# A selective scan that takes two channel tiles per step instead of one

## The chip, the cores and the metric

The kernel runs on one core of a Trainium2 chip. Its metric is device time in microseconds: three runs of the kernel before took 5609.75, 5609.93 and 5616.93 us (median 5609.93). One further execution was recorded by the hardware profiler; its trace is what the tables below are read from.

The core's engines work side by side, each on its own list of instructions, in that list's order: PE multiplies matrices into PSUM, DVE works element by element, ACT does functions of one input (exponentials, copies), POOL issues the scattered transfers, SP issues nearly all others. They wait for each other by semaphores.

## The reference

One decoder block over x of 8 sequences of 512 tokens of width 512, all in float32, with a layernorm after each of three parts: a state-space layer, cross attention (16 heads of 32, keys and values from a context), and a mixture of 32 experts (4 per token, 640 places each) with a shared expert. The change is in the state-space layer. Per channel d of 1024 and state n of 16:

```python
dt = softplus(dt @ dt_proj_w + dt_proj_b)
dA = exp(A * dt)                      # decay, per channel, state and token
dBx = dt * B * x_main                 # what a token adds
h = dA_t * h + dBx_t                  # the recurrence over the tokens
y_t = sum over n of h * C_t
out = res_scale * ((y + x_main * D) * silu(z)) @ out_proj_w + x
```

A = -exp(A_log); B and C come from a product of x_main with x_proj_w, and x_main is a causal convolution of four taps followed by silu.

## The kernel before, in words

`layers` works in 16 chunks: 8 sequences of two chunks of T = 256 tokens. A chunk has 1024 channels in 8 tiles c of 128, taken as four pairs q (tiles 2q and 2q+1); the 16 states are in four groups g of NG = 4. A step is one (q, g, i), i being the tile of the pair, so a chunk has 32 steps k and the program 512. A tile of a step is laid out so that each partition holds two channels j by two states m; `dt` and `dt*x` are copied into that form by the DMAs of `prepare` (the tiles `both`).

One step does this, in program order:

- `bcast` (L374), in the first step of a pair: four transfers that fetch the next group's B and C rows to all partitions (tiles `bc`, four buffers).
- `carry` (L439): takes an h buffer, 4 rows of 257, from a pool of four, and ACT copies the last state (or zeros, `nothing`) into column 0.
- `decays` (L433) for the *next* step: four exponentials of 256 columns on ACT into one of two `das` tiles.
- `scan` (L446): on DVE the product of `dt*x` with B over 1024 columns (L449), then one `tensor_tensor_scan` through all 4 x 257 columns (L453; column 0 of each decay row is 0, so each row starts from its carried state), and, in the first chunk of a sequence, a copy of the last column to `state` (L455).
- work of other parts (below).
- `collect` (L457): DVE multiplies h by C in place (L470), and PE sums over states with four products with the matrix `twice` into `py` (L474).

The other work is hung on step numbers: `back` (the output projection of the chunk before) at k = 1 and 2, `gate_x` at 3 to 6, `prepare` of the next pair at k % 8 == 3 (PE product, seven ACT operations, four DVE operations, two more on ACT, eight transfers `both<-dt` and `both<-dtx`), `convolve` at 12, 15, 18 and 21, `x_proj` of the next chunk at 24. Beside these runs a list `side`: the attention and routing of the sequence before (`units`), with weights in time that spread it evenly over 64 steps. Each piece has up to three parts (PE, then ACT or DVE, then more), and a part is emitted when the next piece has been (`do`, `settle`).

So the program order is written by hand, with weights. The compiler's list scheduler then reorders each engine's list within the dependencies, so products of a later step may come before other work. At run time each engine keeps its list's order. A pool's buffer is handed out again when its last reader has finished; for h that is PE's L474.

After `layers` come `experts` and a last layernorm (`finish`), which the change does not touch.

Of the kernel before, what the change touches and what calls it, by code (L numbers as in the profile page):

```python
# [7 lines left out]
F32 = mybir.dt.float32  # L8
I32 = mybir.dt.int32
U8 = mybir.dt.uint8  # L10
AF = mybir.ActivationFunctionType
# [5 lines left out]
P = 128  # L17
# [9 lines left out]
T = 256  # L27
# [54 lines left out]
def layers(ctx, tc, a, x1d, filld, based, xbuf):  # L82
# [73 lines left out]

    conv_tail = cp.tile([P, CC, 3], F32, name="l_conv_tail")
    state = cp.tile([P, CC, NST // NG, NG], F32, name="l_state")
    nothing = cp.tile([P, NG, 1], F32, name="l_nothing")
    nc.gpsimd.memset(nothing, 0.0)  # L160
    das = [cp.tile([P, NG, T + 1], F32, name=f"l_da{i}") for i in range(2)]
    for da in das:
        nc.gpsimd.memset(da[:, :, 0:1], 0.0)

# [23 lines left out]
        channel_multiplier=0,  # L188
    )

    early = cp.tile([P, SC, E], F32, name="l_early")
    nc.gpsimd.iota(
        early, pattern=[[0, SC], [-1, E]], base=E, channel_multiplier=0, allow_small_or_imprecise_dtypes=True
    )
    first = cp.tile([P, SC, E], F32, name="l_first")
    nc.gpsimd.iota(
        first, pattern=[[0, SC], [CAP, E]], base=-SLOTS, channel_multiplier=0, allow_small_or_imprecise_dtypes=True
    )

    taken = cp.tile([P, SC + 1, E], F32, name="l_taken")  # L200
    nc.gpsimd.memset(taken, 0.0)
# [172 lines left out]
    def bcast(f, g):  # L374

        got = []
        for r0 in (g * NG, NST + g * NG):
            t = bcp.tile([P, NG // 2, T], F32, tag="bc", name="bc")
            for r in range(2):
                n0 = r0 + r * NG // 2  # L380
                nc.sync.dma_start(
                    t[r * HP : (r + 1) * HP], f["scr"][n0 : n0 + NG // 2, :].partition_broadcast(HP)
                )
            got.append(t.unsqueeze(1).to_broadcast([P, 2, NG // 2, T]))
        return got

    def prepare(q, f):
# [42 lines left out]

        return exponentials

    def decays(c, g, dt, da):  # L433

        for n in range(NG):
            j, m = n // 2, n % 2
            nc.scalar.activation(da[:, n, 1:], dt[:, c % 2, j, :], AF.Exp, scale=aneg[:, c, j, g, m : m + 1])  # L437

    def carry(t, c, g):  # L439

        last = state[:, c, g].unsqueeze(2)
        h = p3.tile([P, NG, T + 1], F32, tag="h", name="h", bufs=4)
        nc.scalar.copy(h[:, :, 0:1], last if t else nothing)  # L443
        return h

    def scan(t, c, g, dtx, bc, da, h):  # L446

        steps = h.rearrange("p (j m) t -> p j m t", j=2)[:, :, :, 1:]
        nc.vector.tensor_tensor(  # L449
            steps, dtx[:, c % 2].unsqueeze(2).to_broadcast([P, 2, NG // 2, T]), bc[0], ALU.mult  # L450
        )
        flat = h.rearrange("p n t -> p (n t)")
        nc.vector.tensor_tensor_scan(flat, da.rearrange("p n t -> p (n t)"), flat, 0.0, ALU.mult, ALU.add)  # L453
        if t < S // T - 1:
            nc.vector.tensor_copy(state[:, c, g].unsqueeze(2), h[:, :, T : T + 1])  # L455

    def collect(c, g, h, bc, py, f):  # L457


        if g == 0:  # L460
            for j in range(2):
                nc.tensor.matmul(
                    py[j * HP : (j + 1) * HP, c % 2, :],
                    ident[:, j * HP : (j + 1) * HP],
                    f["xs"][c // 2][:, c % 2, :],
                    start=(c % 2 == 0),
                    stop=False,
                )
        steps = h.rearrange("p (j m) t -> p j m t", j=2)[:, :, :, 1:]
        nc.vector.tensor_tensor(steps, steps, bc[1], ALU.mult)  # L470
        for m in range(NG // 2):
            for j in range(2):
                s = (g, m, c % 2)
                nc.tensor.matmul(  # L474
                    py[j * HP : (j + 1) * HP, c % 2, :],
                    twice,
                    h[:, j * 2 + m, 1:],
                    start=False,
                    stop=(s == (NST // NG - 1, NG // 2 - 1, 1)),
                )  # L480
# [63 lines left out]
    def choose(b, x2t, pl, st):  # L544
# [13 lines left out]
        square = [P, SC, G, G]  # L558
        other = gs.unsqueeze(2).to_broadcast(square)
        own = gs.unsqueeze(3).to_broadcast(square)  # L560
        eq = gm.tile(square, F32, tag="g_eq", name="g_eq")
        nc.vector.tensor_tensor(eq, other, own, ALU.is_equal)
        nc.vector.tensor_tensor(eq, eq, lower.unsqueeze(1).to_broadcast(square), ALU.mult)
        gt = gm.tile(square, F32, tag="g_gt", name="g_gt")
        nc.vector.tensor_tensor(gt, other, own, ALU.is_gt)
        nc.vector.tensor_tensor(gt, gt, eq, ALU.add)
        nc.vector.tensor_reduce(rank.unsqueeze(3), gt, AX.X, ALU.add)
# [455 lines left out]
    for i, (b, t) in enumerate(chunks):  # L1023
# [8 lines left out]
        for k, (q, g, ci) in enumerate(steps):  # L1032
            if ci == 0:
                if (q, g) != (CC // 2 - 1, NST // NG - 1):
                    bcn = bcast(f, (g + 1) % (NST // NG))
                else:
                    bcn = bcast(nf, 0) if after else None
            h = carry(t, 2 * q + ci, g)

            if k + 1 < len(steps) or after:  # L1040
                nq, ng, ni = steps[(k + 1) % len(steps)]
                decays(2 * nq + ni, ng, (f if k + 1 < len(steps) else nf)["ready", nq][0], das[(n + 1) % 2])
            scan(t, 2 * q + ci, g, f["ready", q][1], bc, das[n % 2], h)
            n += 1
            if k % 8 == 0:
                if k:
                    gated(q - 1, f, py)
# [9 lines left out]
            if k == 7:  # L1057
                dry()
                silu(f["zs"])
            if k % 8 == 3:  # L1060
                if q + 1 < CC // 2:
                    do(prepare, q + 1, f)
                elif after:
                    do(prepare, 0, nf)
# [354 lines left out]
```

## Time and profile before

| what | us |
|---|---|
| median of three runs | 5609.93 |
| profiled execution, time | 5620.06 |
| profiled execution, span of the core | 5617.3 |
| mean granted TensorE clock | 0.934 of full |

Busy time of each engine by stage (us):

| window | PE | DVE | ACT | POOL | granted clock |
|---|---|---|---|---|---|
| 0 to 280 (constants, first chunk) | 166.79 | 215.60 | 135.35 | 21.44 | 0.83 |
| 280 to 3640 (scan with the side work) | 2899.31 | 3029.36 | 1901.24 | 242.17 | 0.93 |
| 3640 to 5617 (last attention, experts) | 1822.51 | 1106.57 | 555.57 | 282.46 | 0.96 |

How to read what follows: DVE is VectorE, ACT ScalarE, POOL GpSimd, SP the queue that issues transfers; PE's weight loads stand apart as PEld. A group's line names line, engine, operation, output and inputs by the program's tile names, shapes, and how often; behind it busy us, the mean ns of one, the engine's idle us just before them, and what ended most of it. A line of waits gives who waited for whom, the total us, how often, the longest. Matmuls are recorded twice each (two passes). A busy engine is not always at its best rate, and the idle time of an engine that is not the bottleneck costs nothing.

### The profile page before, as it was taken

The numbers are of one execution on the slowest core, as the hardware profiler recorded it, in microseconds if no ns is written. First come the engines' busy times: TensorE is split into PE (matmuls) and PEld (weight loads), VectorE is DVE, ScalarE is ACT, GpSimd is POOL, SyncE is SP. The second block draws the span as 40 slices with busy tenths as digits, with TensorE's granted clock in tenths as the row PEclk, the third lists the DMA queues.
The fourth block names the chain that finished last, engine by engine and source line by source line (L and its number), as shares of the span: only waits on it lengthen the run. The fifth ranks groups of instructions, "written<-read, shape, count | busy, mean of one in ns | idle before, by whom it ended". The sixth has DMA issues, their size and how long they took to land. (4 is left out here: it accounts for less than half of the span.)

```text
span 5617.3 us, 60406 instructions
## 1 busy us (share of the span) xinstructions
PE 4888.6 (87%) x19752; PEld 2725.6 (49%) x19752; DVE 4351.5 (77%) x5738; ACT 2592.2 (46%) x5480; POOL 546.1 (10%) x424
## 2 busy tenths in 40 slices
PE   5667888888888988888888898879899999999994
PEld 3333344434433434443443443333577777777773
DVE  5988888989889998898989899854555655555554
ACT  4454555655556555565545656523122222222223
POOL 0000002001100200200010020010111111111111
PEclk8778999999999999999999999989899999999997
DMA  6777345434534534543463453431444444444444
GB/s 207 215 219 201 99 129 177 128 112 130 189 107 113 190 107 122 177 132 106 124 204 94 125 183 110 115 118 45 137 124 126 124 124 119 125 126 124 120 117 138
DMA packets 560426, 769.83 MB, mean 137 GB/s; under 512 B 135754, under 2 KB 268394, under 8 KB 560112
## 3 DMA queue, kind: packets, MB, share of 16 engines
q1 hardware_dynamic: 522608, 680.70, 40.2%
q0 software_dynamic: 33280, 76.90, 7.0%
q10 hardware_dynamic: 4224, 8.39, 0.4%
q8 instruction: 156, 2.56, 0.2%
q14 instruction: 158, 1.29, 0.1%
HBM read 508.68 MB, written 165.05 MB: 120 GB/s over the span
## 5 line engine op out<-in xcount | busy, mean ns | idle before, releaser
L437 ACT ACTIVATE l_da<-both,l_aneg 128x256 f32<-128x256 f32 x2048 | 888.4, 499 | 801.8 <-DVE h L453 759.7
L453 DVE TENSOR_TENSOR_SCAN h<-l_da,h 128x1028 f32<-128x1028 f32 x512 | 1171.2, 2295 | 48.5 <-ACT h L443 26.4
L474 PE MATMUL py<-h,l_twice 128*64 128x256 f32 x4096 | 628.1, 420 | 217.4 <-DVE h L470 217.3
L449 DVE TENSOR_TENSOR h<-both,bc 128x1024 f32<-128x1024 f32 x512 | 619.2, 1216 | 97.2 <-PE py L474 45.4
L470 DVE TENSOR_TENSOR h<-h,bc 128x1024 f32<-128x1024 f32 x512 | 623.5, 1220 | 6.0
L474 PEld LDWEIGHTS py<-h,l_twice 128*64 128x64 f32 x4096 | 295.3, 147 | 587.6 <-DVE h L470 260.7
L766 PE MATMUL ps_s<-l_ka,l_qa 64*128 64x512 f32 x1024 | 317.1, 699 | 142.9 <-DVE mx L768 142.7
L1199 PE MATMUL ps_h<-xT,w 128*128 128x320 f32 x1536 | 435.6, 433 | 0.0
L1279 POOL DMA_INDIRECT based<-y,xe x160 | 250.5, 1565 | 1317.2 <-ACT y L1302 579.9
L768 DVE TENSOR_REDUCE mx<-ps_s 128x2 f32<-128x1024 f32 x256 | 310.8, 1217 | 83.7 <-PE ps_s L766 82.9
L1220 DVE TENSOR_TENSOR hT<-ps_h,p 128x320 f32<-128x320 f32 x128 | 62.9, 492 | 374.7 <-PE ps_h L1199 374.6
L1199 PEld LDWEIGHTS ps_h<-xT,w 128*128 128x128 f32 x1536 | 292.4, 191 | 118.4 <-issue 0.8
L792 PE MATMUL ps_t<-l_qa,l_ka 64*128 64x512 f32 x1024 | 302.0, 654 | 15.8 <-ACT eT L796 11.9
L796 ACT ACTIVATE eT<-ps_t 128x1024 f32<-128x1024 f32 x256 | 259.1, 1013 | 111.9 <-PE ps_t L792 111.5
L808 PE MATMUL po<-eT,l_va 128*64 128x512 f32 x1024 | 279.2, 623 | 23.0 <-ACT raw L820 19.0
L1199 PE MATMUL ps_h<-t,s 128*128 128x320 f32 x1024 | 286.1, 432 | 0.0
L641 POOL DMA_INDIRECT xbuf<-x2t,dest x128 | 216.7, 1693 | 622.1 <-DVE dest L635 583.7
L305 PE MATMUL ps_z<-xnT,wm 128*128 128x256 f32 x1024 | 246.3, 395 | 31.2 <-DMA wm<-in_in_proj_w 28.4
L503 PE MATMUL po<-wm,zs 128*128 128x512 f32 x512 | 246.7, 634 | 13.0 <-DMA wm<-in_out_proj_w 8.5
L703 PE MATMUL ps_p<-x2T,wa 128*128 128x512 f32 x512 | 244.7, 627 | 11.1 <-DVE hT L883 9.1
L305 PE MATMUL ps_x<-xnT,wm 128*128 128x256 f32 x1024 | 245.3, 393 | 1.4 <-ACT xnT L294 1.1
L305 PEld LDWEIGHTS ps_z<-xnT,wm 128*128 128x128 f32 x1024 | 196.2, 196 | 83.7 <-ACT l_da L437 27.1
(225 smaller groups left out, 7397.0 us busy)
## 6 DMA issues: line engine op xcount, KB each, us to landing
bc<-scr SPq DMA_DIRECT2D x1024, 128.0 KB
w<-in_w SPq DMA_DIRECT2D x96, 1024.0 KB
wm<-in_in_proj_w SPq DMA_DIRECT2D x128, 512.0 KB
xbuf<-zero SPq DMA_DIRECT2D x32, 1362.5 KB
xe<-xbuf SPq DMA_DIRECT2D x32, 1362.5 KB
both<-dt SPq DMA_DIRECT2D x256, 128.0 KB
both<-dtx SPq DMA_DIRECT2D x256, 128.0 KB
wm<-in_out_proj_w SPq DMA_DIRECT2D x64, 512.0 KB
```

The source lines that it names most:

```text
L305: nc.tensor.matmul(ps[:, i, :], w[:, dc, i * P : (i + 1) * P], f["xnT"][:, dc, :], start=(dc == 0), stop=(dc == DC - 1),)
L437: nc.scalar.activation(da[:, n, 1:], dt[:, c % 2, j, :], AF.Exp, scale=aneg[:, c, j, g, m : m + 1])
L449: nc.vector.tensor_tensor(steps, dtx[:, c % 2].unsqueeze(2).to_broadcast([P, 2, NG // 2, T]), bc[0], ALU.mult)
L453: nc.vector.tensor_tensor_scan(flat, da.rearrange("p n t -> p (n t)"), flat, 0.0, ALU.mult, ALU.add)
L470: nc.vector.tensor_tensor(steps, steps, bc[1], ALU.mult)
L474: nc.tensor.matmul(py[j * HP : (j + 1) * HP, c % 2, :], twice, h[:, j * 2 + m, 1:], start=False, stop=(s == (NST // NG - 1, NG // 2 - 1, 1)),)
L766: nc.tensor.matmul(ps[:, j, :], qa[r, lt * P : (lt + 1) * P], ka[r, :], start=True, stop=True)
L768: return lambda: nc.vector.tensor_reduce(mx[:, lt, :].unsqueeze(2), ps, AX.X, ALU.max) and None
L792: nc.tensor.matmul(ps[:, j, :], ka[r, kc * P : (kc + 1) * P], qa[r, :], start=True, stop=True)
L796: nc.scalar.activation(eT, ps, AF.Exp)
L808: nc.tensor.matmul(po[j * 2 * HD : (j + 1) * 2 * HD, :], va[:, kc, i, j * HD : (j + 2) * HD], eT[:, j, :], start=(kc == 0), stop=(kc == SC ...
L1199: nc.tensor.matmul(ps, w[:, n, r * P : (r + 1) * P], x[:, n, :], start=not more and n == 0, stop=n == 1, skip_group_check=more,)
```

## The change

A step's scan work is done once for both tiles of a pair. The h tile and the two decay tiles hold 8 rows of 257 instead of 4; h has two buffers instead of four. In the first of a pair's two steps `carry` copies 8 columns, `decays` writes the eight decays of the *next pair's* step, and `scan` does one product with B over 2048 columns, one scan through 2056 and one copy of 8 states. The second step has none of these. `collect` stays as it was, once for each tile, on its half of h, after that step's other work. `prepare` moves from k % 8 == 3 to k % 8 == 2. To make room, the constants `early` and `first` are held once and read as broadcasts over the four row tiles, and `g_eq` and `g_gt` of the routing take one buffer of the pool "row" in place of two of their own.

```diff
-    das = [cp.tile([P, NG, T + 1], F32, name=f"l_da{i}") for i in range(2)]
+    das = [cp.tile([P, 2 * NG, T + 1], F32, name=f"l_da{i}") for i in range(2)]
...
-    early = cp.tile([P, SC, E], F32, name="l_early")
+    early = cp.tile([P, E], F32, name="l_early")
...
+    early = early.unsqueeze(1).to_broadcast([P, SC, E])
...
-    def decays(c, g, dt, da):
-
-        for n in range(NG):
-            j, m = n // 2, n % 2
-            nc.scalar.activation(da[:, n, 1:], dt[:, c % 2, j, :], AF.Exp, scale=aneg[:, c, j, g, m : m + 1])
-
-    def carry(t, c, g):
-
-        last = state[:, c, g].unsqueeze(2)
-        h = p3.tile([P, NG, T + 1], F32, tag="h", name="h", bufs=4)
-        nc.scalar.copy(h[:, :, 0:1], last if t else nothing)
+    def decays(q, g, dt, da):
+
+        for i in range(2):
+            for n in range(NG):
+                j, m = n // 2, n % 2
+                nc.scalar.activation(
+                    da[:, i * NG + n, 1:], dt[:, i, j, :], AF.Exp, scale=aneg[:, 2 * q + i, j, g, m : m + 1]
+                )
+
+    def carry(t, q, g):
+
+        h = p3.tile([P, 2 * NG, T + 1], F32, tag="h", name="h", bufs=2)
+        nc.scalar.copy(h.rearrange("p (i n) t -> p i n t", i=2)[:, :, :, 0], last(q, g) if t else none)
         return h
 
-    def scan(t, c, g, dtx, bc, da, h):
-
-        steps = h.rearrange("p (j m) t -> p j m t", j=2)[:, :, :, 1:]
+    def last(q, g):
+        return state[:, 2 * q : 2 * q + 2, g]
+
+    def scan(t, q, g, dtx, bc, da, h):
+
+        steps = h.rearrange("p (j m) t -> p j m t", m=NG // 2)[:, :, :, 1:]
+        both = [P, 4, NG // 2, T]
         nc.vector.tensor_tensor(
-            steps, dtx[:, c % 2].unsqueeze(2).to_broadcast([P, 2, NG // 2, T]), bc[0], ALU.mult
+            steps,
+            dtx.rearrange("p i j t -> p (i j) t").unsqueeze(2).to_broadcast(both),
+            bc[0].to_broadcast(both),
+            ALU.mult,
         )
         flat = h.rearrange("p n t -> p (n t)")
         nc.vector.tensor_tensor_scan(flat, da.rearrange("p n t -> p (n t)"), flat, 0.0, ALU.mult, ALU.add)
         if t < S // T - 1:
-            nc.vector.tensor_copy(state[:, c, g].unsqueeze(2), h[:, :, T : T + 1])
+            nc.vector.tensor_copy(last(q, g), h.rearrange("p (i n) t -> p i n t", i=2)[:, :, :, T])
...
+        h = h[:, c % 2 * NG : (c % 2 + 1) * NG]
...
-        eq = gm.tile(square, F32, tag="g_eq", name="g_eq")
+        both = p3.tile([P, D], F32, tag="row", name="g_eq").rearrange("p (n j g h) -> p n j g h", n=2, j=SC, g=G)
+        eq, gt = both[:, 0], both[:, 1]
...
-            h = carry(t, 2 * q + ci, g)
-
-            if k + 1 < len(steps) or after:
-                nq, ng, ni = steps[(k + 1) % len(steps)]
-                decays(2 * nq + ni, ng, (f if k + 1 < len(steps) else nf)["ready", nq][0], das[(n + 1) % 2])
-            scan(t, 2 * q + ci, g, f["ready", q][1], bc, das[n % 2], h)
-            n += 1
+            if ci == 0:
+                h = carry(t, q, g)
+
+                if k + 2 < len(steps) or after:
+                    nq, ng, _ = steps[(k + 2) % len(steps)]
+                    decays(nq, ng, (f if k + 2 < len(steps) else nf)["ready", nq][0], das[(n + 1) % 2])
+                scan(t, q, g, f["ready", q][1], bc, das[n % 2], h)
+                n += 1
...
-            if k % 8 == 3:
+            if k % 8 == 2:
                 if q + 1 < CC // 2:
                     do(prepare, q + 1, f)
```

More of the change, by code (lines that the diff above doesn't have):

```diff
@@ L158, in layers @@
     state = cp.tile([P, CC, NST // NG, NG], F32, name="l_state")
-    nothing = cp.tile([P, NG, 1], F32, name="l_nothing")
-    nc.gpsimd.memset(nothing, 0.0)
-    das = [cp.tile([P, NG, T + 1], F32, name=f"l_da{i}") for i in range(2)]
+    none = cp.tile([P, 2, NG], F32, name="l_none")
+    nc.gpsimd.memset(none, 0.0)
+    das = [cp.tile([P, 2 * NG, T + 1], F32, name=f"l_da{i}") for i in range(2)]
     for da in das:
@@ L189, in layers @@
     )
-    early = cp.tile([P, SC, E], F32, name="l_early")
[L192 to L198, printed above, removed]
+    early = cp.tile([P, E], F32, name="l_early")
+    nc.gpsimd.iota(early, pattern=[[-1, E]], base=E, channel_multiplier=0, allow_small_or_imprecise_dtypes=True)
+    early = early.unsqueeze(1).to_broadcast([P, SC, E])
+    first = cp.tile([P, E], F32, name="l_first")
+    nc.gpsimd.iota(first, pattern=[[CAP, E]], base=-SLOTS, channel_multiplier=0, allow_small_or_imprecise_dtypes=True)
+    first = first.unsqueeze(1).to_broadcast([P, SC, E])
     taken = cp.tile([P, SC + 1, E], F32, name="l_taken")
@@ L383, in bcast @@
                 )
-            got.append(t.unsqueeze(1).to_broadcast([P, 2, NG // 2, T]))
+            got.append(t.unsqueeze(1))
         return got
@@ L468, in collect @@
                 )
+        h = h[:, c % 2 * NG : (c % 2 + 1) * NG]
         steps = h.rearrange("p (j m) t -> p j m t", j=2)[:, :, :, 1:]
-        nc.vector.tensor_tensor(steps, steps, bc[1], ALU.mult)
+        nc.vector.tensor_tensor(steps, steps, bc[1].to_broadcast([P, 2, NG // 2, T]), ALU.mult)
         for m in range(NG // 2):
@@ L560, in choose @@
         own = gs.unsqueeze(3).to_broadcast(square)
-        eq = gm.tile(square, F32, tag="g_eq", name="g_eq")
+        both = p3.tile([P, D], F32, tag="row", name="g_eq").rearrange("p (n j g h) -> p n j g h", n=2, j=SC, g=G)
+        eq, gt = both[:, 0], both[:, 1]
         nc.vector.tensor_tensor(eq, other, own, ALU.is_equal)
         nc.vector.tensor_tensor(eq, eq, lower.unsqueeze(1).to_broadcast(square), ALU.mult)
-        gt = gm.tile(square, F32, tag="g_gt", name="g_gt")
         nc.vector.tensor_tensor(gt, other, own, ALU.is_gt)
```

## The prediction

> **What bounds the kernel now.** I read the page first (span, busy shares, the 40 slices), then the busy times by stage, then VectorE's groups in the stage that the change touches, then its instructions in order of time, and last the waits. The chain of work that ended last only names the closing layernorm, so it carries nothing here.
>
> ```profile
> span 5617.3 us, 60406 instructions
> ...
> PE 4888.6 (87%) x19752; PEld 2725.6 (49%) x19752; DVE 4351.5 (77%) x5738; ACT 2592.2 (46%) x5480; POOL 546.1 (10%) x424
> ...
> PE   5667888888888988888888898879899999999994
> ...
> DVE  5988888989889998898989899854555655555554
> ...
> PEclk8778999999999999999999999989899999999997
> ```
>
> The 77% of DVE is a mean of two stages: DVE stands at 8 or 9 tenths up to slice 26 and at half after it. By stage:
>
> ```profile
> 280.00:3640.00 3360.00, 2899.31 (x11832) 1383.86 (x11830) 3029.36 (x3456) 1901.24 (x4021) 242.17 (x186) 0.93 0.48 142
> 3640.00:5617.00 1977.00, 1822.51 (x7252) 1252.12 (x7248) 1106.57 (x2034) 555.57 (x1147) 282.46 (x195) 0.96 0.44 119
> ```
>
> The columns are window, length, then PE, PEld, DVE, ACT and POOL busy. The scan lives in the first row: DVE 3029 of 3360 us (90%), PE 2899 (86%), so DVE leads and PE follows closely. The second row (attention of the last sequence, experts) is untouched.
>
> ```profile
> L453 DVE TENSOR_TENSOR_SCAN h<-l_da,h 128x1028 f32<-128x1028 f32 x500 | 1143.8, 2295 | 46.2 <-ACT h L443 26.4 <-ACT l_da L437 4.2
> L470 DVE TENSOR_TENSOR h<-h,bc 128x1024 f32<-128x1024 f32 x500 | 608.9, 1221 | 6.0
> L449 DVE TENSOR_TENSOR h<-both,bc 128x1024 f32<-128x1024 f32 x500 | 604.8, 1216 | 95.4 <-PE py L474 45.4 <-DMA both<-dtx 25.0 <-DMA bc<-scr 11.2
> L455 DVE COPY l_state<-h 128x4 f32<-128x4 f32 x256 | 42.1, 166 | 2.9
> ```
>
> These four groups are 2400 us of it. A duration is not what an instruction costs, though, because the next one may start before it ends:
>
> ```profile
> 2086.49 2.30 DVE L453 TENSOR_TENSOR_SCAN h<-l_da,h 128x1028 f32<-128x1028 f32 x1
> 2088.82 1.22 DVE L470 TENSOR_TENSOR h<-h,bc 128x1024 f32<-128x1024 f32 x1
> 2089.97 1.22 DVE L768 TENSOR_REDUCE mx<-ps_s 128x2 f32<-128x1024 f32 x1
> 2091.10 1.22 DVE L449 TENSOR_TENSOR h<-both,bc 128x1024 f32<-128x1024 f32 x1
> 2092.42 2.30 DVE L453 TENSOR_TENSOR_SCAN h<-l_da,h 128x1028 f32<-128x1028 f32 x1
> 2094.63 1.20 DVE L768 TENSOR_REDUCE mx<-ps_s 128x2 f32<-128x1024 f32 x1
> ```
>
> First column start, second duration. Where the next one needs the result, the product takes 1.32 us from start to start (2091.10 to 2092.42) and the scan 2.33 (2086.49 to 2088.82); where it does not, 1.13 to 1.15 and 2.21.
>
> ```profile
> DVE h L449 <- PE py L474: 45.4, 27, 3.7
> ...
> DVE h L453 <- ACT h L443: 26.4, 16, 2.0
> DVE h L449 <- DMA both<-dtx: 25.0, 14, 7.1
> ...
> PE py L474 <- DVE h L470: 134.2, 40, 7.9
> ```
>
> Total us, times, longest. DVE rarely waits, and when the product does, it is because PE has not finished with the h buffer.
>
> **Price of size.** Rows of 512, 1024 elements take 0.685 and 1.216 us, so an element costs 1.04 ns and the rest, 0.153 us, is per instruction. A scan element costs 2.08 ns (2.295 less 0.153, over 1028). From start to start, taking medians over the trace, the fixed part is 0.068 us where the next instruction is independent (product 1.135, scan 2.209), 0.254 for a product whose scan follows at once (1.321), 0.19 for a scan whose result is wanted at once (2.33).
>
> **Change, part by part, against the profiled execution's 5620.06 us** (10.1 above the median of 5609.93; I take the same difference off both).
>
> 1. Products with B: 512 become 256. In the trace of before 209 are followed at once by a scan and 303 are not: 209 x 0.254 + 303 x 0.068 = 73.7 us of fixed cost. In the compiled order of the changed kernel it is 132 and 124: 33.5 + 8.4 = 41.9. Saved: 32.
> 2. Scans: 512 become 256. Before, 226 are followed by a copy or product of h (mean 2.297, so 0.155 over the elements) and 286 by other work: 35.0 + 19.2 = 54.2. After, 112 and 144: 21.3 + 9.6 = 30.9. Saved: 23.
> 3. Copies of the state: 256 become 128. Before, mostly 0.204 us where a product with C follows (108 times), 0.07 to 0.12 otherwise: 32. After, 68 and 60: 18. Saved: 14.
>
> Together DVE loses 69 us. Both ends: 0.068 x (256 + 256 + 128) = 44 if everything overlapped, 0.153 x 512 + 0.16 x 128 = 99 if durations counted in full. Element work is the same, and the product with C stays in halves. DVE leads the stage, so I count the 69 on the path.
>
> The Trainium skill (Perfetto Trace Analysis, Optimizing Scalar/DVE Operations) gives about 60 ns per DVE instruction and says that profiled latency is about twice that, because half overlaps; by it the saving would be 640 x 0.06 = 38 us instead of my 69. The same section says that where an engine causes bubbles on others, breaking instructions up can help, which speaks against this change; the PE waits on L470 (134 us) are such bubbles.
>
> 4. ACT: 256 carry copies (0.19 us) go, 49 us of ACT. ACT is busy 1901 of 3360 us: no gain on the path. Decays now come eight at a time (8 x 0.499 = 4.0 us). They wait for the scan two pairs back. The DVE work standing between that scan's end and the scan that needs them has a median of 20 us in the new order and a minimum of 12 (before: 10 and 5, for 2.0 us). So covered: 0. Queued behind a waiting batch on ACT are the exponentials of attention, PSUM copies and the next carry; if the cover fails, the row "scan waits for l_da" (4.2 us) grows, and I bound that by doubling: 0 to +4. The first batch of the program is uncovered: +2.
> 5. The h buffers: four halves become two wholes, same bytes. A product now needs both halves of the pair two back to be through PE, where before it needed one half. DVE work (by the rows' durations, in the compiled order) between the last product with C of that pair and the new product: median 15 us, 67 of 256 pairs under 12, 32 under 10, nine under 4 (before: median 20, 17 of 512 under 10). ACT's carry waits on the same buffer (its rows show 205 us of waiting on PE) and the scan behind it. Low end 0: the cover shrinks at every quantile, so I see no gain. High end: the 32 pairs under 10 us at the longest wait seen (3.7) is 118, less the present 45, is +73; the scan's wait on the carry doubled is +26. PE needs 8 matmuls at 0.3 us (148 ns for each of two recorded passes) after those products, mostly inside 15 us, so nearer the low end: +25.
> 6. `prepare` moves from the fourth step of eight to the third: 2 matmuls, 9 activations, 4 DVE operations, 8 transfers on SP, past the `bc` fetches and any weight piece that SP issues in that step. The distance to the first decays that use it is unchanged (they moved a step too), but the product that reads dtx stays, so the 25 us of "L449 waits for both<-dtx" get a step (3360/500 = 6.7 us) more: -25 to 0, and half, -12. What goes behind it is `bc` (11 us of waits in three cases): 0 to +11, I take 0 since `bc` is fetched a pair ahead. At chunk ends it sits two steps behind `x_proj` instead of three; PE waits for xd 0.5 us in all now: 0.
> 7. `early`/`first` as broadcasts, `g_eq`/`g_gt` in the "row" pool: rows with a broadcast operand (L582, 291 ns) and without (L585, 286) are equal: 0. The row buffer can be held by an outgoing transfer; `k`, in the same pool, waits 2.5 us in all for that: 0 to +3, I take 0.
>
> Sum: -69 + 2 + 25 - 12 = -54, so 5566 for the profiled execution and **5556 for the median**.
>
> The clock: in the trace, PE idled from 1965 to 1970 (1.35 of 5 us busy) at a granted 0.80, and the next 5 us were granted 0.52, with 1.00 on both sides. Wider DVE blocks (product and scan now 6.9 us against 3.7) give PE longer gaps; the stage has 31 gaps over 3 us now. I put no term on it: PE has 461 us of slack here. The Trainium skill (TensorE: Matmul & The Clock Gate, Part 1) says an idle window of about 3.4 us halves the clock until a busy one has passed; by it 100 more such gaps would cost PE 100 x 1.7 = 170 us, a third of that slack.
>
> **Rivals.**
> - A, all gain: no new waits on PE. For: DVE waits 45 us on that buffer now. Against: the cover. -69 - 12 = 5529, at full durations and with all of item 6, 5486.
> - B, PE sets the pace: its 2899 busy us plus waits for DVE in larger lumps eat the gain; or the fixed cost grows with size and only the copies go. Then -14 - 12 + 25, about 5609; 5586 to 5621. For: PE at 86% against DVE at 88% after. Against: DVE's waits on PE and ACT together are small.
> - C, slower: the two-deep h buffer makes DVE wait. It decides from (69 + 12)/256 = 0.32 us of added wait per pair. 67 pairs under 12 us of cover at half the longest wait (1.85) are 124, less 45, plus 26 on the carry: +105 against -81, 5634; at the full 3.7, 5758. For: PE's share of work per pair is uneven (`back`, `x2T` steps). Against: 27 waits in 500 steps now.
>
> **How the numbers follow.** Forecast (5525 to 5585): 0.46. A: 0.16. B: 0.14. C: 0.24. A difference of 0.2% (11 us) is about what can be told here. Faster is the forecast, A and 0.06 of B: 0.68; same is the rest of B, 0.08; slower is C, 0.24. The range is 5495 to 5640: below lies the last part of A (0.04), above half of C (0.12). The likeliest case's own range is 5525 to 5585.
>
> **What would show it.** Right: the product with 2048 columns at about 2.28 us and the scan with 2056 at 4.44, DVE busy in the scan stage 70 to 100 us lower, the dtx wait below 25. Item 5: "L449 waits for PE py" (now at the wide product) between 45 and 120. Wrong: that row, or the carry row, over 130 us; PE idle in the stage well over 461; a granted clock there below 0.90; or scans well over 4.6 us.

## The result and the profile after

The changed kernel takes 5616.74 us (median of 20 runs, 5608.12 to 5630.07), the kernel before, run beside it on the same chip, 5615.06 us (20 runs, 5609.75 to 5622.26). The ratio is 1.0006, 95% interval 1.0000 to 1.0012: no change that can be told. Forecast was 5556.

The profiled execution of the changed kernel took 5630.07 us, the longest of the 20 and 13 above their median; small differences between the two traces are read with that in mind, and beside the trace of the control described under the h buffers below, which issues the same instructions in the same order and took 5617.09. Its page, span and busy shares, and the slices of PE, DVE and the granted clock:

```profile
span 5628.4 us, 59369 instructions
...
PE 4884.2 (87%) x19752; PEld 2733.3 (49%) x19752; DVE 4299.8 (76%) x5098; ACT 2494.3 (44%) x5186; POOL 546.4 (10%) x424
...
PE   5667889888888988888898898879899999999994
...
DVE  5988888999889888988888988854456555555554
...
PEclk8888999999998999999999899989899999999997
```

The busy times of the scan stage of the changed kernel (window, length, PE, PEld, DVE, ACT, POOL, granted clock, DMA share, GB/s):

```profile
280.00:3640.00 3360.00, 2888.20 (x11809) 1383.99 (x11807) 2969.44 (x2877) 1804.61 (x3746) 235.25 (x186) 0.93 0.48 141
```

DVE is busy 60 us less than before in that window (2969 against 3029), ACT 97 us less, PE 11 us less, and PE's clock is as before. (Of ACT's 97 us, 38 are carry copies and 51 are loads of its function tables, 82 instead of 122 at 1.28 us; the prediction did not have the latter.) So the work did shrink. DVE's groups of the changed kernel, over the whole program:

```profile
L460 DVE TENSOR_TENSOR_SCAN h<-l_da,h 128x2056 f32<-128x2056 f32 x256 | 1135.8, 4437 | 14.3 <-ACT h L443 2.1 <-ACT l_da L436 0.5
L478 DVE TENSOR_TENSOR h<-h,bc 128x1024 f32<-128x1024 f32 x512 | 611.8, 1219 | 5.3 <-DVE l_state L462 0.6
L453 DVE TENSOR_TENSOR h<-both,bc 128x2048 f32<-128x2048 f32 x256 | 584.3, 2287 | 140.0 <-PE py L482 75.9 <-DMA both<-dtx 48.2 <-DMA bc<-scr 8.8
L776 DVE TENSOR_REDUCE mx<-ps_s 128x2 f32<-128x1024 f32 x256 | 310.7, 1217 | 126.3 <-PE ps_s L774 123.8
L337 DVE SCALAR_TENSOR_TENSOR xs<-xp,l_cw,xs 128x256 f32<-128x256 f32 x384 | 166.8, 479 | 62.4 <-ACT xs L329 61.3
```

The wide product takes 2.287 us and the wide scan 4.437, as two of the old ones less one fixed part each. The saving is real; the last column shows where it went. DVE's waits in the scan stage of the changed kernel (who waited for whom, us in total, times, longest):

```profile
DVE h L453 <- PE py L482: 75.9, 62, 3.8
DVE mx L776 <- PE ps_s L774: 53.9, 35, 3.9
DVE xs L337 <- ACT xs L329: 50.4, 26, 7.3
DVE h L453 <- DMA both<-dtx: 43.5, 7, 7.8
DVE g_m L558 <- ACT g_sc L557: 36.2, 6, 9.9
```

and the rows of before that answer to the second and third, which the prediction did not show, with the largest row of ACT:

```profile
DVE xs L339 <- ACT xs L331: 33.0, 21, 4.7
...
DVE mx L768 <- PE ps_s L766: 13.1, 10, 2.2
...
ACT l_da L437 <- DVE h L453: 701.1, 291, 5.3
```

Every one of the five is longer than before (45, 13, 33, 25 and, for `g_m`, nothing): some 160 us more in those and in `k` (L696, 1 to 18 us). Four others got shorter by some 83 us (the scan's wait on the carry fell from 26 to 1). Summed over the trace from the first scan to the last, DVE's gaps went from 341 to 406 us (392 in the control's trace), while its busy time went from 3300 to 3247: the 53 us are given back as gaps.

Two of the longer rows are not the scan's at all: `mx` is attention's maximum, `xs` the convolution of the next chunk. Both stand on work of ACT, directly or through PE. ACT's waits in the same stage of the changed kernel:

```profile
ACT l_da L436 <- DVE h L460: 472.9, 128, 8.7
ACT u L400 <- PE ps_dt L390: 293.4, 48, 17.3
ACT h L443 <- PE py L482: 162.8, 79, 6.0
...
ACT eT L804 <- PE ps_t L800: 107.7, 66, 4.4
```

A batch of decays waits for a scan less often than before but for up to 8.7 us at a time (5.3 before); the average is 3.7 us against 2.4. In total ACT waits less for scans than before (473 us against 701), so the size of the row alone does not tell what it costs. How that reaches DVE is seen at one place that comes back in every sequence. ACT, DVE and PE of the changed kernel in order of time (start, duration; in brackets the idle time before, and what ended it):

```profile
2109.95 2.90 ACT L436 ACTIVATE l_da<-both,l_aneg 128x256 f32<-128x256 f32 x7 [4.28 <-DVE h L460]
2112.75 1.00 ACT L804 ACTIVATE eT<-ps_t 128x1024 f32<-128x1024 f32 x1
2113.66 0.50 ACT L436 ACTIVATE l_da<-both,l_aneg 128x256 f32<-128x256 f32 x1
...
2105.48 4.43 DVE L460 TENSOR_TENSOR_SCAN h<-l_da,h 128x2056 f32<-128x2056 f32 x1
...
2118.70 1.23 DVE L776 TENSOR_REDUCE mx<-ps_s 128x2 f32<-128x1024 f32 x1 [3.94 <-PE ps_s L774]
...
2112.36 1.13 PE L774 MATMUL ps_s<-l_ka,l_qa 64*128 64x512 f32 x4 [2.88 <-DVE mx L776]
2113.81 1.94 PE L800 MATMUL ps_t<-l_qa,l_ka 64*128 64x512 f32 x4 [0.32 <-ACT eT L804]
2115.68 1.92 PE L816 MATMUL po<-eT,l_va 128*64 128x512 f32 x4
2117.53 1.13 PE L774 MATMUL ps_s<-l_ka,l_qa 64*128 64x512 f32 x4
```

ACT stands 4.28 us until the wide scan has ended, because the decays at the head of its list go into the tile that this scan reads. Behind them on the list is the exponential `eT`, whose input was there by 2109.5 at the latest (PE did nothing for the 2.88 us up to 2112.36). It starts 7.3 us after the scan's start; PE's next `ps_t` waits for it, then `po`, then `ps_s`, and DVE waits 3.94 us for that. The late exponential is the smaller part of this wait: PE stands 0.32 us for `eT`, and its next two bursts of four matmuls take 1.94 and 1.92 us, where they take 1.02 and 1.08 at full clock (see the last section). In all seven sequences that have this place `eT` starts 7.3 us after the scan's start; DVE's wait is 2.29 us in the two where the granted clock stayed at 1.00, and 3.80 to 3.94 in the five where it dropped.

Over the whole stage PE's waits for `eT` are 68 us in the changed kernel and 14 in the one before (the changed kernel's rows first):

```profile
PE ps_t L800 <- ACT eT L804: 35.7, 36, 3.0
...
PE po L816 <- ACT eT L804: 21.3, 10, 3.9
...
PE ps_s L774 <- ACT eT L804: 11.2, 14, 1.4
```

```profile
PE ps_t L792 <- ACT eT L796: 10.2, 17, 1.1
...
PE po L808 <- ACT eT L796: 3.6, 4, 1.4
```

### The profile page after: what moved, and what is told of

It reads as the page before. It is cut to its first block, busy times and chain, and to the rows that moved or that the text cites. A ratio compares the mean times of both kernels' runs of the same rounds, so it can differ in the third digit from the quotient of the medians.

```text
span 5628.4 us, 59369 instructions
## 1 busy us (share of the span) xinstructions
PE 4884.2 (87%) x19752; PEld 2733.3 (49%) x19752; DVE 4299.8 (76%) x5098; ACT 2494.3 (44%) x5186; POOL 546.4 (10%) x424
## 5 line engine op out<-in xcount | busy, mean ns | idle before, releaser
L460 DVE TENSOR_TENSOR_SCAN h<-l_da,h 128x2056 f32<-128x2056 f32 x256 | 1135.8, 4437 | 14.3 <-ACT h L443 2.1
L436 ACT ACTIVATE l_da<-both,l_aneg 128x256 f32<-128x256 f32 x2048 | 867.4, 498 | 563.8 <-DVE h L460 517.2
L453 DVE TENSOR_TENSOR h<-both,bc 128x2048 f32<-128x2048 f32 x256 | 584.3, 2287 | 140.0 <-PE py L482 75.9
L478 DVE TENSOR_TENSOR h<-h,bc 128x1024 f32<-128x1024 f32 x512 | 611.8, 1219 | 5.3 <-DVE l_state L462 0.6
L816 PE MATMUL po<-eT,l_va 128*64 128x512 f32 x1024 | 294.1, 646 | 27.8 <-ACT eT L804 22.9
```

Source lines behind the costliest of these rows:

```text
L436: nc.scalar.activation(da[:, i * NG + n, 1:], dt[:, i, j, :], AF.Exp, scale=aneg[:, 2 * q + i, j, g, m : m + 1])
L453: nc.vector.tensor_tensor(steps, dtx.rearrange("p i j t -> p (i j) t").unsqueeze(2).to_broadcast(both), bc[0].to_broadcast(both), ALU.mult,)
L478: nc.vector.tensor_tensor(steps, steps, bc[1].to_broadcast([P, 2, NG // 2, T]), ALU.mult)
L816: nc.tensor.matmul(po[j * 2 * HD : (j + 1) * 2 * HD, :], va[:, kc, i, j * HD : (j + 2) * HD], eT[:, j, :], start=(kc == 0), stop=(kc == SC ...
```

## The experiments

Two theories stood at first: the product's and the scan's shape costs what it saves (or the moved `prepare` does), against: DVE's saving is taken back by waits. Later, when waits were found, the question was which: the h buffers (two whole ones), or the decays on ACT. In what follows "held" means that every engine's list is chained to the order that the compiler gave the kernel it is derived from, so that an edit shows without a new order; otherwise the compiler orders the lists anew. Medians of five rounds; the kernel before, beside them, took 5615 to 5620. A ratio is to that kernel; a difference is between medians, and where the ratios give another size, both are said.

**`prepare` moved back, and moved alone.**

```diff
 changed kernel                      kernel before
-            if k % 8 == 2:          -            if k % 8 == 3:
+            if k % 8 == 3:          +            if k % 8 == 2:
```

> The changed kernel with prepare put back to the fourth step of eight (k % 8 == 3); all else as changed. Theory S (the new stalls come from particular waits that the moved step brought: the product waits 43.5 us for both<-dtx where it was 25.0, and ACT stands 293 us at the first operation of prepare, u, waiting for PE, where it was 16 us): those rows go back to about 25 and under 50 us, and the time falls by 20 to 40 us, to 5577 to 5597. Theory P (PE, not DVE, sets the pace in most of the stage, so waits only change places): within 10 us of the changed kernel's 5617. Theory G (the grain of whole pairs costs what the wide instructions save): also about 5617, since the grain is the same.

> The kernel before with the one edit that moves prepare from the fourth step of eight to the third; lists rescheduled. In the changed kernel that edit is worth 80 us. If it is good in itself (dtx lands a step before its use), the time falls by 10 to 30 us, 5587 to 5607. If the changed kernel only needs it because its decays are asked for a step earlier, within 10 us of 5617.

Measured: `prepare` back in the changed kernel 5697.65, ratio 1.0141 [1.0127, 1.0156], 81 us slower than the changed kernel, which none of the theories had; moved alone in the kernel before 5605.71, 0.9985 [0.9976, 0.9994], 10 us faster. So undoing the move does not bring the gain back. Both kernels have a new order of the lists, so neither number is the price of the move alone, and why the first is so much stays open. Moved alone, it made ACT's row "u waits for PE ps_dt" grow from 14 to 126 us and DVE's "product waits for both<-dtx" from 25 to 51, while the time fell.

**Pair tiles, but the work in halves (new order).**

```diff
+        for i in range(2):
+            nc.vector.tensor_tensor(steps[:, 2 * i : 2 * i + 2], dtx[:, i]..., bc[0]..., ALU.mult)
+            flat = h[:, i * NG : (i + 1) * NG].rearrange("p n t -> p (n t)")
+            nc.vector.tensor_tensor_scan(flat, da[:, i * NG : (i + 1) * NG]..., flat, 0.0, ALU.mult, ALU.add)
```

and, in the second kernel, the wide product in the pair's first step, a half scan and four decays in each step.

> The changed kernel's pair tiles (h twice as large in two buffers, decays eight at a time, prepare at the third step), but the product with B and the scan issued as two halves each, one after the other: the wide instructions are undone, the grain is kept. DVE gets back 32 + 23 = 55 us of fixed cost at most (its halves can be interleaved, so 25 to 55). Theory G: DVE is still the pace, and the grain alone costs some 70 us: 5617 + 25 to 55, so 5642 to 5672. Theory P: DVE's cost does not matter: 5610 to 5625.

> Between the two kernels: one product with B over 2048 columns in the first step of a pair, but the scan in halves of 1028, one in each step, four decays in each; h in two buffers of a pair; lists rescheduled. DVE keeps the 32 us of the products and loses the 23 + 14 of scans and copies. If long blocks on DVE (product and scan 6.9 us in one piece) cause the lost gain, this is faster than both, by 20 to 35 us: 5582 to 5600. If the whole-pair buffer does, no gain: 5610 to 5640.

Measured: 5614.45 (0.9992 [0.9984, 1.0001]) and 5621.73 (1.0013 [1.0004, 1.0022]). With 256 products and 256 scans more than the changed kernel, the first is no slower. So in these orders the width as such bought nothing end to end; this does not yet say why.

**What a microsecond of DVE or of PE is worth.** The product with C over 224 of 256 columns (68 us less on DVE), and PE's products with `twice` over 224 (an estimated 79 us less on PE; these products' own busy time fell by 63 and 59), each in both kernels.

```diff
-        nc.vector.tensor_tensor(steps, steps, bc[1], ALU.mult)
+        short = steps[:, :, :, : T - 32]
+        nc.vector.tensor_tensor(short, short, bc[1][:, :, :, : T - 32], ALU.mult)
```
```diff
-                    py[j * HP : (j + 1) * HP, c % 2, :],
+                    py[j * HP : (j + 1) * HP, c % 2, : T - 32],
...
-                    h[:, j * 2 + m, 1:],
+                    h[:, j * 2 + m, 1 : T - 31],
```

> The kernel before, its product with C shortened to the first 224 of 256 tokens of each row (the last 32 tokens' states are summed without C, so their y is wrong). DVE loses 128 elements x 1.04 ns x 512 = 68 us, the same as the change was to save, with no change of grain, count or buffers. Theory G: DVE sets the pace, so 50 to 70 us faster: 5545 to 5565. Theory P: 0 to 20 us faster: 5595 to 5615.

> The changed kernel with the same shortened product with C (224 of 256 tokens; the last 32 tokens' y is wrong): DVE loses another 68 us. Theory G (waits are set by the two-deep buffers of whole pairs): DVE's saving is partly eaten, 20 to 50 us faster than 5617: 5567 to 5597. Theory P: 0 to 15 us faster, 5602 to 5617. If both b_c224 and this one gain their full 68, neither theory holds and the changed kernel's extra waits are an accident of its order.

> The kernel before with the product with C over 224 of 256 tokens (the last 32 tokens' y is wrong), and now every engine's list held in exactly the order of the kernel before, so that only the durations change: DVE loses 68 us. Rescheduled, the same edit was 33 us faster. Theory P (PE and DVE pace the stage together; DVE's cost counts only where PE is not the later one): 15 to 40 us faster. Theory G (DVE is the pace; whole-pair grain ate the gain): 55 to 70 faster. Theory O (the order of the lists decides, and the scheduler's new order was a worse fit): between, but equal in size to what the changed kernel gains in its own held order.

> The changed kernel with the same shortened product with C, every list held in the order of the changed kernel. Rescheduled, it was 41 us slower than the kernel before although DVE had less to do. Theory O: most of that was the new order, so held it is faster than the changed kernel's 5617, by as much as the kernel before gains: 5577 to 5600. Theory P: 0 to 20 us faster. Theory G: 20 to 50 faster, less than the kernel before.

> The kernel before with PE's products with the matrix twice over 224 of 256 tokens (the last 32 tokens' y lacks the states), order held: PE loses about 632 x 32/256 = 79 us, DVE nothing. Theory P: 20 to 50 us faster. Theories G and O (DVE is the pace in a given order): 0 to 20 us faster.

> The changed kernel with the same shortened PE products, order held. Theory P: the changed kernel stands on PE more than the one before, so it gains more, 40 to 70 us. Theory G: h buffers come free sooner, which whole pairs need, 20 to 40 us. Theory O: as the kernel before.

| edit | kernel before | changed kernel |
|---|---|---|
| product with C cut, new order | 5585.38, 0.9944 [0.9931, 0.9957] | 5657.55, 1.0077 [1.0064, 1.0090] |
| product with C cut, held | 5563.40, 0.9900 [0.9886, 0.9914] | 5594.49, 0.9954 [0.9939, 0.9968] |
| PE's products cut, held | 5607.23, 0.9977 [0.9969, 0.9986] | 5626.35, 1.0015 [1.0006, 1.0024] |

In the order held, 68 us off DVE are worth 56 in the kernel before and 22 in the changed one (29 by the ratios): DVE sets the pace before and largely no longer does after. Nothing says that PE sets it instead: shorter products bought 12 in the kernel before, and in the changed one the time did not fall (1.0015, with an interval that overlaps the changed kernel's own 1.0006). That test is weaker than planned, since PE's busy time in the stage fell by only 30 and 33 us (last section). And the same instructions in a new order are 22 us (before) and 63 us (changed) slower than in the order held. An order is thus worth tens of microseconds, and every comparison across orders carries that.

**The h buffers.** A third whole buffer needs room; two weights are cut to a part of themselves for it, and a control has only that cut.

```diff
-    w_x = const("w_x", [P, CC, RANK + 2 * NST], rows(a["x_proj_w"]))
-    w_dt = const("w_dt", [RANK, DI], a["dt_proj_w"])
+    w_x = const("w_x", [P, 1, RANK + 2 * NST], rows(a["x_proj_w"])[:, 0:1])
+    w_dt = const("w_dt", [RANK, P], a["dt_proj_w"][:, 0:P])
...
-        h = p3.tile([P, 2 * NG, T + 1], F32, tag="h", name="h", bufs=2)
+        h = p3.tile([P, 2 * NG, T + 1], F32, tag="h", name="h", bufs=3)
```

> The changed kernel with three h buffers of a whole pair instead of two, every list held in the order of the changed kernel. Room for the third comes from the weights of dt and x_proj, of which one tile is kept and used for all channels (their output is wrong; the instructions and shapes are the same). If the two-deep h buffer is the cause of the lost gain, the rows 'wide product waits for PE py' (76 us) and 'carry waits for PE py' nearly vanish and the time falls by 50 to 80 us, to 5540 to 5565. If the waits only move to other places (the round trips of DVE, PE and ACT in one fixed order), 0 to 25 us.

> Control for the two kernels with narrowed weights: the changed kernel, lists held, two h buffers and two decay tiles, only the weights of dt and x_proj narrowed. Every theory: within 8 us of the changed kernel's 5617.

Measured: control 5618.12 (1.0007 [0.9995, 1.0018]), so the cut weights cost nothing; three buffers 5598.22 (0.9970 [0.9959, 0.9982]). The row "L453 waits for PE py" (76 us) goes, but `mx` (45 in the control to 68) and `xs` (54 to 63) wait longer instead, and 20 us are gained against the control. The two-deep h buffer is a part, not the cause.

**The wide instructions in halves, order held.** The same halves as above, but at the places where the wide ones stood; then the scan alone, then the product alone.

> The changed kernel with each wide product and each wide scan issued as two halves back to back, in exactly the place the wide one has in the changed kernel's lists; buffers and all else are held. DVE gets 256 x 0.068 us back for the products and at least as much for the scans, 35 to 55 us. In the changed order 68 us off DVE were worth 22, a third. If that holds for work put on, too, 10 to 25 us slower than the changed kernel, about 5627 to 5642; if DVE is the pace, 35 to 55 slower, 5652 to 5672; if DVE has slack, no change, 5617.

> The changed kernel, lists held, only the wide scan issued as two halves in its place; the product stays wide. Both halves of both were 46 us faster than the changed kernel. Theory R (ACT's eight decays of the pair after next may overwrite a decay tile only when the scan that reads it has ended; a half scan frees half of it 2.2 us sooner, and what stands behind the decays on ACT comes sooner): this one keeps most of the 46 us, 5570 to 5590. Theory D (a half of a product or scan hides the pause that DVE makes before an instruction that needs the last one's result): the gain is shared, about 5590 to 5600 here and for the halved products.

> The changed kernel, lists held, only the wide product issued as two halves in its place; the scan stays wide. Theory R: nothing that another engine waits for ends sooner, within 10 us of 5617. Theory D: DVE's pause between product and scan (0.186 us, 132 times: 25 us) is filled for 0.068 us each 256 times (17 us), so 5605 to 5615, or, with the scans' part, 5590 to 5600.

| halved | us | ratio | "decays wait for the scan" (us, times, longest) |
|---|---|---|---|
| nothing (changed kernel) | 5616.74 | 1.0006 [1.0000, 1.0012] | 472.9, 128, 8.7 |
| scan | 5585.35 | 0.9937 [0.9924, 0.9950] | 269.7, 164, 6.4 |
| product and scan | 5570.80 | 0.9922 [0.9908, 0.9936] | 270.0, 160, 6.4 |
| product | 5649.73 | 1.0059 [1.0046, 1.0072] | 478.9, 127, 8.8 |

Halving the scan, which costs DVE fixed time (0.07 to 0.19 us in each of 256 places), gains 31 us (39 by the ratios): its first half frees four decay rows two microseconds sooner. With both halved the kernel is 46 us faster than the changed one and 44 faster than the one before, although it issues 512 more DVE instructions than the changed one; all three expectations had it slower or equal. DVE's gaps from the first scan to the last are 333 us in it. The halved product alone costs 33, against both theories; 17 of them are busy time of DVE (3265 us from the first scan to the last, against 3247), and the rest stays open. The rule in the Trainium skill (Perfetto Trace Analysis, Optimizing Scalar/DVE Operations) that breaking instructions up can let work complete sooner is what the halved scan shows, and the halved product does not. The page gives it for an engine that is not saturated, a condition that the prediction left out; here DVE was 88% busy (2969 of 3360 us), and for the scan it held.

**A third decay tile.** If the decays' wait is the cause, it must go with another tile to write into, at the scan's full width.

```diff
-    das = [cp.tile([P, 2 * NG, T + 1], F32, name=f"l_da{i}") for i in range(2)]
+    das = [cp.tile([P, 2 * NG, T + 1], F32, name=f"l_da{i}") for i in range(3)]
...
-                    decays(nq, ng, ..., das[(n + 1) % 2])
-                scan(t, q, g, f["ready", q][1], bc, das[n % 2], h)
+                    decays(nq, ng, ..., das[(n + 1) % 3])
+                scan(t, q, g, f["ready", q][1], bc, das[n % 3], h)
```

In the changed kernel it needs the cut weights of the control; in the kernel before the third (half-size) tile fits as it is.

> The changed kernel, lists held, wide instructions, with three decay tiles instead of two (room from the narrowed weights of dt and x_proj, so their output is wrong). Theory R: the decays no longer wait for the scan just before (473 us of ACT's waiting in 128 waits go), and the time falls as with halves, by 30 to 60 us. If ACT's waits cost nothing, within 10 us of 5617.

> The kernel before (half-size tiles), with three decay tiles instead of two and every engine's list held to its own compiled order. Nothing is left out. In the trace of before the exponentials of the decays wait 701 us for scans, 291 times, in batches of four. Theory R (the widened batch is what hurts: with two tiles of eight rows the batch stands at the head of ACT's list until a whole wide scan has ended, and what is queued behind it is late): a batch of four is released twice as often and at half the distance, so the third tile is worth much less here than the 57 us that it is worth in the changed kernel: ACT's row goes, the total falls by 0 to 20 us (5595 to 5615). Rival (two decay tiles are simply too few, in either form, and the change has nothing to do with it): the same 40 to 60 us are gained here (5555 to 5575), and the widening as such is then again worth nothing against it.

Measured: changed kernel 5560.64, 0.9905 [0.9890, 0.9919], 57 us under its control; kernel before 5594.82, 0.9955 [0.9941, 0.9968], 25 under itself. DVE's waits, then ACT's, in the scan stage of the changed kernel with three tiles:

```profile
DVE h L453 <- PE py L482: 54.1, 56, 4.0
DVE h L453 <- DMA both<-dtx: 48.5, 14, 7.6
DVE g_m L558 <- ACT g_sc L557: 28.8, 6, 5.1
DVE xs L337 <- ACT xs L329: 26.2, 12, 7.4
DVE mx L776 <- PE ps_s L774: 25.4, 28, 1.7
...
ACT u L400 <- PE ps_dt L390: 280.9, 47, 18.2
ACT h L443 <- PE py L482: 225.9, 96, 8.0
ACT eT L804 <- PE ps_t L800: 192.5, 102, 4.8
```

The decays' row on ACT is gone. DVE's `mx`, `xs` and the product's wait for PE together are 74 us shorter (180 to 106), and DVE's gaps fall from 406 to 333 us; against the control's trace, which differs in nothing but the third tile, it is 69 us (175 to 106) and 392 to 333. PE's waits for `eT` fall from 70 us in the control to 38. `eT` now waits for PE more (192 us): it is ready before its input, as it should be. The same place as above, ACT, DVE and PE in order of time:

```profile
2068.03 2.89 ACT L436 ACTIVATE l_da<-both,l_aneg 128x256 f32<-128x256 f32 x7
2070.82 1.00 ACT L804 ACTIVATE eT<-ps_t 128x1024 f32<-128x1024 f32 x1
...
2067.96 4.43 DVE L460 TENSOR_TENSOR_SCAN h<-l_da,h 128x2056 f32<-128x2056 f32 x1
...
2078.94 1.22 DVE L776 TENSOR_REDUCE mx<-ps_s 128x2 f32<-128x1024 f32 x1 [1.70 <-PE ps_s L774]
...
2075.80 1.02 PE L800 MATMUL ps_t<-l_qa,l_ka 64*128 64x512 f32 x4
2076.75 1.08 PE L816 MATMUL po<-eT,l_va 128*64 128x512 f32 x4
```

The decays run during the scan, `eT` starts 2.9 us after the scan's start instead of 7.3, and DVE's wait for `ps_s` is 1.70 us instead of 3.94. So it is in all seven sequences, and together they gain 12 us here (10 against the control): 0.59 us each against the wait of 2.29 at full clock, the rest by the clock. The granted clock of the whole run is 0.942 to 0.944 with three tiles and 0.936 to 0.941 in the control, so a part of the 57 us may come by way of the clock; no run separates it.

In the kernel before the third tile removes more waiting on ACT (701 to 64 us), and gains less than half as much; ACT then waits for the h buffer instead:

```profile
ACT h L443 <- PE py L474: 558.7, 206, 10.1
...
ACT l_da L437 <- DVE h L453: 64.2, 44, 4.0
```

The measured 25 lies between what the two theories expected there (0 to 20, and 40 to 60), nearer the first. Two decay tiles are somewhat too few in the kernel before, and clearly too few in the changed one, where a batch has doubled.

**The same cause, taken away otherwise.** Pair tiles, halves, and a ring of five half-size decay tiles, lists ordered anew.

```diff
-    das = [cp.tile([P, 2 * NG, T + 1], F32, name=f"l_da{i}") for i in range(2)]
+    das = [cp.tile([P, NG, T + 1], F32, name=f"l_da{i}") for i in range(5)]
...
-            l = p1.tile([P, 2, T], F32, tag="l", name="l")
+            l = p1.tile([P, 2, T + 3], F32, tag="xp", name="l")[:, :, 0:T]
```

> The changed kernel with its pair tiles for h, product and scan each done in two halves, and five decay tiles of half the size used in turn instead of two of the whole size (room: the first softplus tile l takes a buffer of the tag xp); the compiler orders the lists anew. Nothing is left out. Theory R: no batch of decays waits for a scan any more, so the row of ACT's decays waiting for the scan goes below 50 us and ACT's other work comes in time; against the 5614 of the same halving with two tiles, 30 to 50 us less (5565 to 5585), give or take some 40 for the new order, which the runs so far have shown to move a kernel of the same instructions by that much. Rival (the order decides, the decays don't): 5600 to 5640 with the row gone.

Measured: 5605.29, 0.9972 [0.9963, 0.9981]. It is 9 us under the same halves with two tiles, and misses both expectations: the row of the decays is still 310 us. The room of half a pair was not enough to empty that row in the new order. Across orders the row is no measure of the time either: it was 345 us in the slowest kernel of all (5697.65) and 701 in the one before. It can be called a cause only within one order, where a single edit takes it away.

## Why the prediction went wrong, point by point

1. **Products, scans, copies (-32, -23, -14).** The prices were right: from start to start, product to its scan 2.38 to 2.39 us (2.387 by the prediction's figures), scan to a use of its result 4.474 (4.475), scan to other work 4.352 (4.350). In sum 59 came, not 69: 53 busy and 6 in gaps under 0.15 us. DVE busy in the scan stage is 60 lower, not 70 to 100. The 10 are in the products: with the waits left out, the time from their start to the next start fell by 23 us, not 32 (scans 24, copies 14). The prediction multiplied the median 1.32 us by all 209 products that a scan follows, and about a fifth of them took 1.135. Its rows of 500, besides, reach from 0 to 3640 us: in the stage itself there are 462 scans, the four groups are 2218 of the 3029 us, and a step takes 7.3 us, not 6.7; the sum does not rest on these.
2. **"DVE leads the stage, so I count the 69 on the path."** True for the kernel before (68 off DVE gave 56), not for the changed one (22). The price of a microsecond was taken from a kernel whose waits the change itself altered.
3. **Item 4, the decays: "So covered: 0", bound 0 to +4. This is the step that failed.** The cover was worked out for the scan that needs the decays, and there it was right: that wait is 0.5 us in the changed kernel. What was queued behind the waiting batch on ACT (the prediction named it: exponentials of attention, PSUM copies, the carry) was given no price of its own. ACT's largest wait, 701 us for scans, stood in the trace of before, and the prediction did not show it. The bound was set on one row, "scan waits for l_da", while the delay shows in others: `xs`, `mx` and the product's wait for PE. A third decay tile, the single edit that takes this wait away, gives 57 us, where the prediction had 0 to 4; the whole miss is 61. In the kernel before the same tile gives 25, so not all of the 57 came with the change (below).
4. **Item 5, the h buffers (+25, 0 to +99).** The row went from 45 to 76, inside the stated 45 to 120, and a third buffer is worth 20: about right. The carry did not get worse: the scan's wait on it fell from 26 to 1 us.
5. **Item 6, `prepare` (-12).** The row it was to shorten grew, 25 to 43.5 us, so the working was wrong. The move alone gives 10 on the kernel before, but in a new order and with that row at 51; that this is near 12 is luck.
6. **Item 7, and the first batch (+2).** No run separates these.
7. **The clock, no term.** PE's gaps over 3 us in the stage rose from 31 to 43, but the mean of the stage is 0.93 in both: right as a mean, though at the place shown above a low grant lengthens the wait.

**Rivals.** A (all gain) is out. B named the band into which the time fell (5586 to 5621) but for PE's pace, which the cut of PE's products speaks against, or a fixed cost that grows with size, which the prices in point 1 exclude. C (h buffer) is a term of 20, not what decides. The rival that happened, ACT's batch standing in front of other engines' work, was not among them. What would show it wrong was listed as the product's row over 130, PE idle well over 461 us, a lower clock or a longer scan; none of these came (PE was idle for 472), and the list missed the rows that did.

**What the account comes to.** DVE from the start of the first scan to the end of the last, summed over the traces, one profiled execution each:

| kernel | length | busy | gaps |
|---|---|---|---|
| before | 3640 | 3300 | 341 |
| changed | 3653 | 3247 | 406 |
| changed, control (two decay tiles) | 3639 | 3247 | 392 |
| before, three decay tiles | 3622 | 3298 | 324 |
| changed, three decay tiles | 3578 | 3245 | 333 |

With two tiles on each side the change saves 53 us of work and adds 65 of gaps (51 by the control's trace); with three on each side it saves 53 and adds 9. By the ratios to the kernel before (0.9955 and 0.9905) the change is then worth 0.5%, 28 us. So 32 us (57 less 25), about half of the 54 forecast, go with the changed kernel. Each of the two prices is shown by a single edit in a held order; by the intervals of the ratios their difference is uncertain by some 13 us. That the doubled batch makes it, and not the other order of the lists, is argued and not shown; the halved scan, which gains 31 us with the same buffers and the same order, speaks for it. The rest is not settled: the two orders that the compiler made differ, the order of one kernel cannot be given to the other, and orders moved identical work by 22 to 63 us.

## What to carry to other kernels

When an instruction is made wider, ask not only whether its inputs come in time but what stands behind the producer while it waits for the old buffer: on an engine that works through its list in order, a longer wait at the head delays everything queued there, for other engines too. The row to look for in the profile before is, by this case, the largest wait of the engine that fills the widened buffer, even if that engine is only half busy; give it one buffer more before widening, or keep the releasing instruction narrow. And judge an edit in the order it had: compare with the lists held, since a new order can move the time by more than the edit.

## What the runs showed of the hardware that I had not expected

Less work on PE lowered the clock that PE was granted. Over 224 of 256 columns the products with `twice` took 63 us less in the kernel before (628 to 565) and 59 less in the changed one (632 to 574), but PE's busy time in the stage fell by only 30 and 33 us. The granted clock of the whole run fell from 0.934 to 0.929 in the kernel before and from 0.937 to 0.930 in the changed one, and all executions agree (0.929 to 0.932 with the cut against 0.933 to 0.938 for the kernel before beside it, and 0.930 to 0.934 against 0.937 to 0.942 for the changed kernel). The stage of the changed kernel with the cut (2854.89 us of PE against 2888.20):

```profile
280.00:3640.00 3360.00, 2854.89 (x11768) 1396.21 (x11770) 2961.76 (x2875) 1801.22 (x3736) 256.39 (x186) 0.92 0.49 141
```

The clock also drops at the place shown: after a stretch in which PE had been busy 0.48 of 3 us, the changed kernel's matmuls were granted 0.57, and four of them took 1.94 us instead of 1.02. The stretch in the changed kernel:

```profile
2109.00:2112.00 3.00, 0.48 (x4) 0.00 (x0) 2.97 (x3) 2.05 (x6) 0.00 (x0) 1.00 0.28 77
2112.00:2114.00 2.00, 1.32 (x6) 0.49 (x8) 1.90 (x3) 2.00 (x5) 0.00 (x0) 1.00 0.01 1
2114.00:2118.00 4.00, 4.00 (x10) 0.77 (x10) 0.76 (x1) 1.53 (x3) 0.00 (x0) 0.57 0.24 70
```

With three decay tiles the corresponding stretch ran at 1.00 throughout, in all seven sequences; with two the clock dropped in five of the seven, and in the control in three. A late exponential can thus cost twice here: the wait itself, and slower matmuls after it. But PE stands 2.88 us before this stretch in every one of these cases, so that pause alone does not make the drop, and with three tiles a drop comes elsewhere: around 2060 us, after a pause of 2.06 us, the bursts `ps_t` and `po` took 1.92 and 1.39 us, where the changed kernel after the same pause (around 2099 us) has 1.02 and 1.08. What decides where the clock drops stays open.
